# A decoder layer with 32 experts on one core: the first tile of each expert is made inside the attention

## The chip, the cores and the metric

The kernel runs on one core of a Trainium2 chip. The metric is the device time of one execution in microseconds (us); the median of several runs is given. Before the change it is 585.74 us (nine runs, 582.87 to 588.87).

## The reference, cut to what matters

The layer takes x of 16 sequences (blocks) of 128 tokens with 256 features, a context of the same shape and a mask, and does three things, each with a layer norm in front and a residual add behind:

```
x = x + latent_attention(layernorm(x))          # 32-wide compressed q, k, v with rotary tables
x = x + cross_attention(layernorm(x), ctx)      # 32 heads of 8, 8 key groups, causal, masked
x = x + experts(layernorm(x))

# experts, over all 2048 tokens
probs = softmax(h @ gate.T)                     # 32 experts
top_vals, top_idx = top_k(probs, 8)
# keep the largest until their renormalised sum reaches 0.8; shares rw sum to 1
for each expert e:                              # FF = 96
    g, u = split(h @ gate_up[e].T)
    out += (silu(g) * u) @ down[e].T * share[:, e]
```

A token keeps at most six experts with these inputs, so most token and expert pairs are zero. All arrays are float32.

## The kernel before

**Attention.** The kernel's first part is a loop over steps `t`, with an order of instructions written out by hand (`tc.manual_schedule`): each engine executes its instructions in the order in which the loop issues them. Four steps make one block of 128 tokens. In a step `step(t)` makes the score tiles (lines 561 to 587): those of the first pass go to `nmz`, the row maxima (DVE, line 581), those of the second pass, which run LAG = 5 steps later, through an exponential to `pt` (ACT, line 586). `maxima(b)` transposes the maxima of block b at t = 4b + 4 and adds them to the queries (`q8m`, DVE, line 536; once per block, so its starts tell the length of four steps). `weigh`, `divide` and `project` follow for the block's two halves (`o_ps` line 594, `ot_ps` line 612, `y_ps` line 634). `values` copies the block's values on POOL (`va`, line 526). Beside them generators are advanced piece by piece with `piece`: latent attention and queries of the next group of four blocks (`ahead`), keys (`side`), and `route` of the finished blocks (`routing`). The last step with scores is t = 66; with `last` = 65 the steps from 65 on are called the tail here. PSUM has three banks with tag `mm` for all small products, four with tag `s` for scores and one with tag `o`.

**Routing.** `route(b0, nb)` works on two blocks at a time, the last four blocks singly. It normalises the tokens (`rs_f`, a power on POOL, line 291; then DVE, PE `tp_f`), makes the logits, the kept experts (`kept`, DVE), and the rank of each token within its expert: a product of `kept` with a triangular matrix plus the running count `before` (`r_ps`, lines 711 to 720). From the rank it takes the row number `di` = expert x 2048 + rank. Then seven indirect DMAs for each block, called sends here (`send`, POOL, line 749), write the token's row of 292 numbers (256 features, token number, 32 shares) to that row of the DRAM buffer `xs`. The sends wait in the list `waiting` and are issued two in a step, three from step 65 on. S11.1 below means block 11, its send number 1.

**SP's queue.** SP issues, in order, loads and the list `bulk`, three in a step from t = 4: zeroing of the first 128 rows of each expert in `xs` (32 transfers of 146 KB), zeroing of the three accumulators `acc` (48), and the weights `wgu` (32). At t = 68 the attention's buffers are given back (`gctx.close`) and `load_down` loads the down weights `wdn` into them.

**Setup of the expert part.** From `before` a short chain (lines 928 to 999) computes how many rows each expert has, the list of tiles beyond the first of each expert (`lrow`, `lexp`), and masks `valid` of the rows in use.

**Expert loop.** The 32 first tiles (rows 0 to 127 of each expert) are written out; the further tiles follow in chunks of CHUNK = 8, nested in `tc.If(n_more > c * CHUNK)`. At each chunk the engines load the tiles' row and expert numbers into registers (line 1093). A tile is 128 rows: SP loads it (`xt`, six ahead), PE transposes it (`x_ps`, line 1031), ACT copies (`xT`), PE multiplies with gate and up weights (`g`, line 1040), ACT makes Silu (`sg`, line 1049), DVE multiplies (`h`, line 1051), PE transposes `h` (line 1058), DVE copies (`hT`, line 1060), PE multiplies with `wdn` (`y_ps`, line 1071), DVE scales with the share (`y`, line 1075), and POOL adds the rows to the accumulator by an indirect DMA, called an add here:

```
nc.gpsimd.indirect_dma_start(
    out=acc[i % NACC],
    out_offset=bass.IndirectOffsetOnAxis(ap=slot[:, i : i + 1], axis=0),
    in_=y, in_offset=None, bounds_check=B * P - 1, oob_is_err=False,
    compute_op=ALU.add,
)
```

`slot` holds the token numbers; for rows not in use it holds 2048, beyond the bound, and such rows are left out (`copy_predicated`, line 1062). Three accumulators take turns. In `step(i, ...)` PE's order is: half of the next tile's gate product, transpose of this `h`, transposes of the tile three ahead, the other half of the next gate product, this tile's `y_ps`.

**End.** The accumulators are read back, added to x and stored (lines 1137 to 1154).

Of the kernel before, what the change touches and what calls it, by code (L numbers as in the profile page):

```python
# [18 lines left out]
P = 128  # L19
B = 16  # L20
# [16 lines left out]
R_TOK, R_SHARE = D, D + 1  # L37
NX = B * P * TOPK // P
CHUNK = 8
AHEAD = 6  # L40
NACC = 3
# [5 lines left out]
C_TRI, C_ONE, C_SEL, C_IOTA, C_EB = 840, 968, 1096, 1608, 1736  # L47
C_TRI32, C_JROW, C_CAND, C_P, C_JX, C_J1, C_P1 = 1768, 1800, 1816, 1820, 1821, 1822, 1823
C_END = 1824
# [15 lines left out]
def decoder_layer(  # L65
# [47 lines left out]
    tab = const.tile([P, C_END], F32, tag="tab", name="tab")  # L113
# [22 lines left out]
    nc.vector.memset(zero, 0.0)  # L136

# [12 lines left out]


# [6 lines left out]
    with ExitStack() as actx:  # L158
# [3 lines left out]
        tbuf = ctx.enter_context(tc.tile_pool(name="tbuf", bufs=2))  # L162
        gctx = ExitStack()
# [39 lines left out]
        wf = apool.tile([P, GB, D], F32, tag="wf", name="wf")  # L203
# [3 lines left out]
        def fold():  # L207
# [38 lines left out]

            for j in range(GB):
                nc.scalar.activation(wf[:, j, :], wf_ps, AF.Copy, scale=bm4[:, j : j + 1])
# [80 lines left out]
        def latent_attention(g):  # L329
# [93 lines left out]
            for j in range(0, GB, 2):  # L423
                y_ps = mm([P, 2, D], f"ly_ps_{g}_{j}")
                for i in range(2):
                    nc.tensor.matmul(  # L426
                        y_ps[:, i, :], lhsT=on, rhs=wf[:, j + i, :], start=True, stop=True
                    )
                nc.vector.tensor_tensor(
                    xres[:, b0 + j : b0 + j + 2, :], y_ps, xres[:, b0 + j : b0 + j + 2, :], ALU.add  # L430
                )
            yield
# [206 lines left out]
        def route(b0, nb):  # L639
# [94 lines left out]
            for j in range(nb):  # L734
# [8 lines left out]
            nc.vector.tensor_tensor(  # L743
                row[:, :, R_SHARE : R_SHARE + NE], kept,
                sk.unsqueeze(2).to_broadcast([P, nb, NE]), ALU.mult,
            )

            def send(j, k):
                sent = nc.gpsimd.indirect_dma_start(  # L749
                    out=xs, out_offset=bass.IndirectOffsetOnAxis(ap=di[:, j, k : k + 1], axis=0),  # L750
                    in_=row[:, j, :], in_offset=None,
                    bounds_check=ROWS - 1, oob_is_err=False,
                )

                tc.declare_no_dep(sent.ins, group="sent", reason="rows are distinct")
                tc.add_to_no_dep_group("sent", sent.ins)


            for j in range(nb):
                for k in range(TOPK - 1):  # L760
                    waiting.append((pair, lambda j=j, k=k: send(j, k)))

        def load_down():
# [7 lines left out]
            return wdp, wdn  # L771
# [34 lines left out]
        nc.sync.dma_start(out=tab[:, C_FIRST:], in_=table[:, C_FIRST:])  # L806
# [18 lines left out]
        bulk = [(xs[e * CAP : e * CAP + P, :], zero) for e in range(NE)]  # L825
# [5 lines left out]
        waiting, rows, turn = [], {}, [0]  # L831

        routed = {b: (b - 1, 2) for b in range(1, B - 4, 2)}
        routed.update({b: (b, 1) for b in range(B - 4, B)})
# [9 lines left out]

        values(0)
        t = 0
        while t < 4 * B + LAG + 8 or behind or routing or fresh:
# [21 lines left out]
            if t == last + 3:  # L869

                gctx.close()
                wdp, wdn = load_down()
# [29 lines left out]
            if t % 4 == 1 and t // 4 + 1 < B:  # L902
                values(t // 4 + 1)
            piece(side)
# [3 lines left out]
            onward()  # L908
            for _ in range(3):
# [3 lines left out]
            for _ in range(2 if t < last else 3):  # L913
# [6 lines left out]
        while waiting:  # L920
            waiting.pop(0)[1]()

# [6 lines left out]
    pcol = tab[:, C_P : C_P + 1]  # L929
    valid = wdp.tile([P, NE + NX], I32, tag="valid", name="valid")  # L930
    n_ps = pp.tile([P, NE], F32, tag="x", name="n_ps")
    nc.tensor.matmul(n_ps, lhsT=ones, rhs=before, start=True, stop=True)
    nc.vector.tensor_scalar(valid[:, 0:NE], n_ps, pcol, None, ALU.is_gt)


# [6 lines left out]
        more[:, 1:16], tab[0:NE, C_JROW + 1 : C_JROW + 16], np2[:, 0:1], None, ALU.is_lt  # L942
    )
    xt = wdp.tile([NE, 1], F32, tag="xt", name="xt")
    nc.vector.tensor_reduce(xt, more[:, 1:16], AX.X, ALU.add)
    t_ps = pp.tile([NE, 2], F32, tag="h", name="t_ps")
    nc.tensor.matmul(
        t_ps[:, 0:1], lhsT=tab[0:NE, C_TRI32 : C_TRI32 + NE], rhs=xt, start=True, stop=True
# [6 lines left out]
    for q in range(4):  # L955
        nc.tensor.matmul(
            q_ps[:, q, :], lhsT=tab[0:NE, C_SEL + q * P : C_SEL + (q + 1) * P], rhs=np2,
# [7 lines left out]
        pos, nq[:, :, 0], tab[:, C_JX : C_JX + 1], 9999.0, ALU.is_le, ALU.mult  # L965
    )
    nc.vector.tensor_tensor(pos, pos, nq[:, :, 1], ALU.add)
    nc.vector.tensor_scalar(pos, pos, tab[:, C_J1 : C_J1 + 1], None, ALU.add)
# [3 lines left out]
    nc.vector.tensor_scalar(low, nq[:, :, 0], -1.0, tab[:, C_JX : C_JX + 1], ALU.mult, ALU.add)  # L972
    nc.vector.tensor_scalar(low, low, float(P), 0.0, ALU.add, ALU.max)
    row0 = wdp.tile([P, 4], F32, tag="row0", name="row0")
    nc.vector.tensor_tensor(row0, tab[:, C_CAND : C_CAND + 4], low, ALU.subtract)
    hot = wdp.tile([P, 4, NX], F32, tag="hot", name="hot")
    for q in range(4):
        nc.vector.tensor_scalar(
            hot[:, q, :], tab[:, C_IOTA : C_IOTA + NX], pos[:, q : q + 1], None, ALU.is_equal
# [8 lines left out]
    nc.vector.tensor_scalar(valid[:, NE:], v_ps, tab[:, C_P1 : C_P1 + 1], None, ALU.is_gt)  # L988
# [12 lines left out]
    slot = wdp.tile([P, NE + NX], I32, tag="slot", name="slot")  # L1001
# [44 lines left out]
    def gate_tile(i):  # L1046
        v = held[i]
        sg = hbuf.tile([P, FF], F32, tag="sg", name=f"sg_{i}")
        nc.scalar.activation(sg, v["g"][:, 0:FF], AF.Silu)  # L1049
        v["h"] = h_ring[i % len(h_ring)]  # L1050
        nc.vector.tensor_tensor(v["h"], v["g"][:, FF:], sg, ALU.mult)  # L1051

    def step(i, e_dve, e_next, row_ahead):
        v = held[i]
        if i + 1 < NT:
# [4 lines left out]
        nc.vector.tensor_copy(hT, h_ps)  # L1060

        nc.vector.copy_predicated(  # L1062
# [201 lines left out]
```

## Time and profile before

| what | value |
|---|---|
| median of nine runs | 585.74 us (582.87 to 588.87) |
| the profiled execution, its own time | 588.16 us |
| its span in the profile | 586.3 us, mean granted clock 0.874 |
| busy: PE, DVE, ACT, POOL | 456.4, 344.7, 175.8, 289.8 us |
| last score step ends, about | 348 us |
| last send starts | 390.8 us |
| adds of the expert loop, first and last start | 404.2 and 552.9 us |
| end of the span | 586.3 us |

The page of a profile describes one execution. Part 2 cuts the span into 40 slices of 14.66 us and gives the busy share of each engine in tenths. Part 5 lists groups of instructions: line, engine, operation, tile written and tiles read, count, then busy us and mean ns of one, then the engine's idle time in front of them and what ended it. A timeline lists instructions in order of time: start, duration in us, engine, line, operation. A window's line has its limits and length and the busy us of PE, weight loads (PEld), DVE, ACT and POOL with the counts, then the mean granted clock of PE, the share of the DMA engines in use, and GB/s.

### The profile page before, as it was taken

To read this page: it belongs to the slowest core of one execution; us is meant where nothing else is said; L and a number is where in the kernel's file an instruction comes from. 1 tells how busy PE (TensorE), PEld (TensorE's weight loads), DVE (VectorE), ACT (ScalarE), POOL (GpSimd) and SP (SyncE) were. 2 spreads that over 40 slices of the span, in tenths; PEclk is the share of its full clock that TensorE was granted. 3 is DMA by queue.
4 is the path that set the end of the run, shared out by engine and by line. 5 is a ranking of instruction groups with operands and counts; after the bars stand their busy time and mean duration, and the time that the engine had idled before them with its cause. 6 is when DMAs were issued, how large, how long until landed. Compare 5 with 4: busy or idle time off the path is not lost.

```text
span 586.3 us, 11946 instructions
## 1 busy us (share of the span) xinstructions
PE 456.4 (78%) x4168; PEld 328.5 (56%) x4168; DVE 344.7 (59%) x1168; ACT 175.8 (30%) x436; POOL 289.8 (49%) x295
## 2 busy tenths in 40 slices
PE   4979788998699888989989883349888888888500
PEld 3646475665466555666756533237666667776400
DVE  3464466576765776665757754624555545665456
ACT  2121033444225433443434341004233222332100
POOL 5711220011264272645446357753888887888700
PEclk9978679999799998996979797558999988998955
DMA  8200267423720718601111119223666577788388
GB/s 268 97 1 28 53 150 183 130 87 87 228 96 30 240 52 186 217 27 33 35 38 37 34 35 244 80 65 105 120 123 122 113 131 136 140 148 141 67 277 297
DMA packets 62743, 68.62 MB, mean 117 GB/s; under 512 B 12962, under 2 KB 57000, under 8 KB 62384
## 3 DMA queue, kind: packets, MB, share of 16 engines
q1 hardware_dynamic: 43232, 50.01, 30.3%
q0 software_dynamic: 16896, 14.98, 14.1%
q10 hardware_dynamic: 2544, 2.75, 1.4%
q8 instruction: 36, 0.59, 0.4%
q14 instruction: 35, 0.29, 0.2%
HBM read 37.48 MB, written 42.50 MB: 136 GB/s over the span
## 4 chain that ended last, share of the span: by engine, by line
PE 40%; DMA 17%; DVE 15%; issue 13%; POOL 11%; SPq 2%; ACT 1%; POOLq 0%; DVEq 0%
POOL xs L749 6%; PE g L1040 6%; DMA acc<-y,slot 6%; PE y_ps L1071 5%; PE s_ps L561 5%; DVE nmz L581 4%; DMA part<-acc 4%; PE o_ps L594 3%; PE s_ps L567 3%; PE q_ps L503 3%; DMA q<-qd 2%; PE x_ps L1031 2%; PE s_ps L574 2%; PE ly_ps L426 1%; DMA xs<-zero 1%
## 5 line engine op out<-in xcount | busy, mean ns | idle before, releaser
L1078 POOL DMA_INDIRECT acc<-y,slot x80 | 123.9, 1549 | 38.7 <-DVE slot L1062 15.4
L749 POOL DMA_INDIRECT xs<-row,di x112 | 110.4, 985 | 36.4 <-issue 29.9
L581 DVE TENSOR_REDUCE nmz<-s_ps 128x4 f32<-128x512 f32 x128 | 82.4, 686 | 66.2 <-PE s_ps L574 63.7
L586 ACT ACTIVATE pt<-s_ps 128x512 f32<-128x512 f32 x128 | 69.5, 595 | 107.3 <-PE s_ps L574 103.3
L1040 PE MATMUL g<-wgu,xT 128*128 (+1 forms) x324 | 83.4, 341 | 10.6 <-issue 10.6
L561 PE MATMUL s_ps<-k,q 32*128 32x128 f32 x1024 | 87.6, 305 | 0.0
L567 PE MATMUL s_ps<-q8m,k 32*128 32x512 f32 x256 | 79.9, 702 | 6.4 <-DVE q8m L536 3.3
L561 PEld LDWEIGHTS s_ps<-k,q 32*128 32x128 f32 x1024 | 74.6, 206 | 3.2 <-issue 1.1
L1033 ACT COPY xT<-x_ps 128x256 f32<-128x256 f32 x83 | 30.9, 372 | 124.0 <-PE x_ps L1031 103.2
L1040 PEld LDWEIGHTS g<-wgu,xT 128*128 128x128 f32 x324 | 58.0, 201 | 17.4 <-issue 13.0
L1071 PE MATMUL y_ps<-wdn,hT 96*128 (+1 forms) x160 | 57.0, 439 | 8.4 <-DVE hT L1060 8.1
L1075 DVE TENSOR_SCALAR y<-y_ps,xt 128x256 f32<-128x256 f32 x80 | 38.7, 484 | 23.1 <-DMA acc<-y,slot 8.4
L1051 DVE TENSOR_TENSOR h<-g,sg 128x96 f32<-128x96 f32 x81 | 20.7, 256 | 38.6 <-ACT sg L1049 28.9
L567 PEld LDWEIGHTS s_ps<-q8m,k 32*128 32x128 f32 x256 | 21.9, 198 | 36.3 <-issue 23.0
L594 PE MATMUL o_ps<-pt,va 128*32 128x512 f32 x256 | 39.0, 686 | 1.8 <-DVE xres L637 1.8
L1031 PE MATMUL x_ps<-tab,xt 128*128 128x128 f32 x166 | 33.8, 287 | 6.1 <-DMA xt<-xs 6.1
L1071 PEld LDWEIGHTS y_ps<-wdn,hT 96*128 96x128 f32 x160 | 25.2, 195 | 21.2 <-DVE hT L1060 14.1
L526 POOL COPY va<-v_sb 128x64 f32<-128x64 f32 x16 | 3.7, 233 | 65.4 <-PE o_ps L594 65.4
L600 ACT ACTIVATE ot<-o_ps,tab 128x512 f32<-128x512 f32 x32 | 22.1, 689 | 31.4 <-PE o_ps L594 31.3
L1060 DVE COPY hT<-h_ps 96x128 f32<-96x128 f32 x80 | 22.7, 284 | 12.4 <-PE h_ps L1058 12.2
L1031 PEld LDWEIGHTS x_ps<-tab,xt 128*128 128x128 f32 x166 | 21.4, 147 | 8.5 <-DMA xt<-xs 6.3
L1058 PE MATMUL h_ps<-tab,h 128*96 128x128 f32 x80 | 22.8, 285 | 0.4 <-DVE h L1051 0.4
(216 smaller groups left out, 696.6 us busy)
## 6 DMA issues: line engine op xcount, KB each, us to landing
xt<-xs SPq DMA_DIRECT2D x86, 146.0 KB
acc<-zero SPq DMA_DIRECT2D x48, 128.0 KB
wgu<-in_w_gu_t SPq DMA_DIRECT2D x32, 192.0 KB
part<-acc SPq DMA_DIRECT2D x24, 256.0 KB
xs<-zero SPq DMA_DIRECT2D x32, 146.0 KB
ct<-in_ctx_t SPq DMA_DIRECT2D x4, 512.0 KB
qd<-qt SPq DMA_DIRECT2D x8, 256.0 KB
out<-xres ACTq DMA_DIRECT2D x8, 256.0 KB
```

The costliest lines, as they stand in the source:

```text
L561: nc.tensor.matmul(s_ps[:, i, :], lhsT=q8[g % 2][rows, i, tok], rhs=k8[g % 2][h][rows, tok], start=(i == 0), stop=True, skip_group_check=True,
L567: nc.tensor.matmul(s_ps, lhsT=k8[g % 2][h][rows, tok], rhs=q8ms[b][rows, :, :], start=True, stop=True, skip_group_check=True,)
L581: nc.vector.tensor_reduce(nmz[b % 2][:, :, 32 * r + h], s_ps, AX.X, ALU.max, negate=True)
L586: nc.scalar.activation(pt, s_ps, AF.Exp)
L594: nc.tensor.matmul(o_ps[32 * r : 32 * r + 32, :, :], lhsT=vaug[b % NVA][:, 4 * h + r, :], rhs=pts.pop((b, h, r)), start=True, stop=True,)
L749: sent = nc.gpsimd.indirect_dma_start(out=xs, out_offset=bass.IndirectOffsetOnAxis(ap=di[:, j, k : k + 1], axis=0), in_=row[:, j, :], in_o ...
L1031: nc.tensor.transpose(x_ps[:, c, :], v["xt"][:, c * P : (c + 1) * P], ident)
L1033: nc.scalar.copy(v["xT"], x_ps)
L1040: nc.tensor.matmul(v["g"], lhsT=v["xT"][:, c, :], rhs=wgu_flat[:, bass.ds(v["e"] * W2 + c * NE * W2, W2)], start=(c == 0), stop=(c == KC - 1),
L1071: nc.tensor.matmul(y_ps, lhsT=hT, rhs=wdn[:, bass.ds(v["e"] * D, D)], start=True, stop=True)
L1075: nc.vector.tensor_scalar(y, y_ps, v["xt"][:, bass.ds(e_dve + R_SHARE, 1)], None, ALU.mult)
L1078: nc.gpsimd.indirect_dma_start(out=acc[i % NACC], out_offset=bass.IndirectOffsetOnAxis(ap=slot[:, i : i + 1], axis=0), in_=y, in_offset=No ...
```

## The change

The first tile of each expert is now made of the tokens of the first eight blocks alone (NEARLY = 8), while the attention still runs.

- When the sends of blocks 0 to 7 are all issued (56 of them), the generator `early()` is advanced once per step, and twice from step 65 on. One advance is a slot (`first_slot`): it loads a tile two slots ahead (`load_first`, with that expert's down weights), and does a part of three tiles: y product and add for tile i - 2, gate products and gating for tile i - 1, transposes for tile i. There are 34 slots for 32 tiles. Here the gate products give `h` already transposed, so that no transpose of `h` is needed. Adds A0 to A31 go to POOL among the sends: A0 in step 51, A13 in step 64, A14 and A15 in step 65, A30 and A31 in step 73.
- After block 7 is routed, the running count is raised to at least 128 for each expert, so that rows of later tokens begin behind the first tile. Blocks 6 and 7 are routed singly for this. The first 256 rows of each expert are zeroed, and the token number in a zeroed row is 2048.
- The expert loop then handles the second tile of each expert (32, written out) and the list of third and later ones, in chunks of CHUNK = 4. `copy_predicated` remains for the listed tiles.
- `gated` takes the place of Silu and one multiply: silu(g) u = 0.5 (tanh(g / 2) + 1) g u, with tanh on ACT and two DVE operations; the factor 0.5 is put into the shares.
- Sends of blocks 0 to 7 go out four in a step after step 32, and all sends four in a step from step 65 on.
- A part of the table is loaded later, with the down weights (`tab2`), and `wf` is a quarter as large: in the latent attention the four `ly_ps` products use 32 rows each in place of 128 rows with zeros.

```diff
+    def add_rows(i, y, tokens):
+        nc.gpsimd.indirect_dma_start(
+            out=acc[i % NACC],
+            out_offset=bass.IndirectOffsetOnAxis(ap=tokens, axis=0),
+            in_=y, in_offset=None, bounds_check=B * P - 1, oob_is_err=False,
+            compute_op=ALU.add,
+        )
+    def gated(pool, g, u, name, h):
+        th = pool.tile(g.shape, F32, tag="th", bufs=2, name=f"th_{name}")
+        nc.scalar.activation(th, g, AF.Tanh, scale=0.5)
+        a = pool.tile(g.shape, F32, tag="ga", bufs=2, name=f"ga_{name}")
+        nc.vector.scalar_tensor_tensor(a, th, 1.0, g, ALU.add, ALU.mult)
+        nc.vector.tensor_tensor(h, a, u, ALU.mult)
...
+            if b0 + nb == NEARLY:
+                yield
+                n_ps = mm([P, NE], "n_ps_first")
+                nc.tensor.matmul(n_ps, lhsT=ones, rhs=before, start=True, stop=True)
+                nc.vector.tensor_scalar(before, n_ps, float(P), 1.0 / P, ALU.max, ALU.mult)
...
-        bulk = [(xs[e * CAP : e * CAP + P, :], zero) for e in range(NE)]
+        bulk = [(xs[e * CAP : e * CAP + 2 * P, :].rearrange("(k p) r -> p k r", p=P),
+                 zero.unsqueeze(1).to_broadcast([P, 2, RW])) for e in range(NE)]
...
+        def load_first(e):
+            v["xt"] = ebuf.tile([P, RW], F32, tag="ext", bufs=SOON + 4, name=f"ext_{e}")
+            load = nc.sync.dma_start(out=v["xt"], in_=xs[e * CAP : e * CAP + P, :])
+            v["wd"] = ebuf.tile([FF, D], F32, tag="ewd", bufs=SOON + 3, name=f"ewd_{e}")
+            nc.sync.dma_start(out=v["wd"], in_=w_dn_t[:, e, :])
...
+        def first_slot(i):
+            if i + SOON < NE:
+                load_first(i + SOON)
+            if i >= 2:
+                v = first_tiles[i - 2]
+                y_ps = mm([P, D], f"ey_ps_{i - 2}")
+                nc.tensor.matmul(y_ps, lhsT=v["h"], rhs=v["wd"], start=True, stop=True)
+                y = ebuf.tile([P, D], F32, tag="ey", bufs=3, name=f"ey_{i - 2}")
+                nc.scalar.mul(y, y_ps, v["xt"][:, R_SHARE + v["e"] : R_SHARE + v["e"] + 1])
+                add_rows(i - 2, y, v["xt"][:, R_TOK : R_TOK + 1].bitcast(I32))
+            both_ps = mm([P, 2, KC, P], f"eg_ps_{i}")
+            if 1 <= i <= NE:
+                v = first_tiles[i - 1]
+                g_ps = both_ps[0:FF, 1, :, :]
+                for f in range(2):
+                    for c in range(KC):
+                        nc.tensor.matmul(
+                            g_ps[:, f, :], lhsT=wgu[:, c, v["e"], f * FF : (f + 1) * FF],
+                            rhs=v["xT"][:, c, :], start=(c == 0), stop=(c == KC - 1))
+                v["h"] = ebuf.tile([FF, P], F32, tag="eh", name=f"eh_{i - 1}")
+                gated(ebuf, g_ps[:, 0, :], g_ps[:, 1, :], f"e{i - 1}", v["h"])
+            if i < NE:
+                v = first_tiles[i]
+                for c in range(KC):
+                    nc.tensor.transpose(both_ps[:, 0, c, :], v["xt"][:, c * P : (c + 1) * P], ident)
+                v["xT"] = ebuf.tile([P, KC, P], F32, tag="exT", name=f"exT_{i}")
+                nc.scalar.copy(v["xT"], both_ps[:, 0, :, :])
...
+            if count[0] == NEARLY * (TOPK - 1):
+                piece(soon, "mm" if t < last + 2 else "s")
...
             onward()
+            if t >= last:
+                piece(soon, "mm" if t < last + 2 else "s")
...
-            for _ in range(2 if t < last else 3):
+            n = 2
+            if t >= last or waiting and 4 * NEARLY < t and waiting[0][0] < NEARLY // 2:
+                n = 4
+            for _ in range(n):
                 if waiting:
                     waiting.pop(0)[1]()
...
-        nc.scalar.activation(sg, v["g"][:, 0:FF], AF.Silu)
-        nc.vector.tensor_tensor(v["h"], v["g"][:, FF:], sg, ALU.mult)
+        gated(hbuf, v["g"][:, 0:FF], v["g"][:, FF:], f"{i}", v["h"])
...
-        nc.vector.copy_predicated(
-            slot[:, i : i + 1], valid[:, i : i + 1], v["xt"][:, R_TOK : R_TOK + 1].bitcast(I32)
-        )
+        if i >= NE:
+            j = i - NE
+            nc.vector.copy_predicated(slot[:, j : j + 1], valid[:, j : j + 1], tokens)
+            tokens = slot[:, j : j + 1]
...
-        row_of = lambda i: i * CAP if i < NE else first_rows[i - NE]
+        row_of = lambda i: i * CAP + P if i < NE else first_rows[i - NE]
```

## The prediction

> **What bounds the kernel now.** I read the page's slices first (part 2), then its costliest groups (part 5), POOL's timeline from 150 us to the end, DVE's timeline and the window sums for the attention, the timeline of all engines in the expert loop, and the waits last. In the slices, 14.66 us each:
>
> ```profile
> PE   4979788998699888989989883349888888888500
> POOL 5711220011264272645446357753888887888700
> PEclk9978679999799998996979797558999988998955
> ```
>
> PE is full until slice 23 (350 us) and POOL is half idle; then PE drops to 3 and its clock to 0.5 while POOL stays at 7; from slice 27 both are at 8. The groups:
>
> ```profile
> L1078 POOL DMA_INDIRECT acc<-y,slot x80 | 123.9, 1549 | 38.7 <-DVE slot L1062 15.4
> L749 POOL DMA_INDIRECT xs<-row,di x112 | 110.4, 985 | 36.4 <-issue 29.9
> ```
>
> In POOL's timeline (start, us, line, operation, idle time before it) these two run without a hole from the attention's last steps on:
>
> ```profile
> 346.44 1.17 POOL L749 DMA_INDIRECT xs<-row,di  x1 [0.20 <-issue]
> ...
> 390.82 0.97 POOL L749 DMA_INDIRECT xs<-row,di  x1 [0.30 <-issue]
> 404.17 1.60 POOL L1078 DMA_INDIRECT acc<-y,slot  x1 [12.38 <-DVE slot L1062]
> ...
> 502.39 1.55 POOL L1078 DMA_INDIRECT acc<-y,slot  x1 [0.30 <-DVE h L1051]
> 504.25 1.55 POOL L1078 DMA_INDIRECT acc<-y,slot  x1 [0.30 <-issue]
> ...
> 552.89 1.55 POOL L1078 DMA_INDIRECT acc<-y,slot  x1 [0.30 <-issue]
> ```
>
> A send holds POOL 0.97 + 0.30 = 1.277 us, an add 1.55 + 0.30 = 1.855 us, whatever the rows hold: L1078's shortest is 1.539, its longest 1.601, and experts with one token are among the 80. The 34 sends from 346.4 to 391.8 are those of steps 65 and later (S11.1 to S15.6). So after step 65 POOL sets the end twice: in the tail (45.4 us) and in the expert loop (404.17 to 552.89 for 79 adds, 1.883 us each).
>
> **Tiles.** The reference's router on its own inputs gives 72 non-empty tiles, 42 beyond an expert's first; in eights that is 48, and 32 + 48 = 80 is the x80 above. After, an expert holds max(rows of the first 1024 tokens, 128) plus the rest: 31 third or later tiles, 32 in fours. So 32 early tiles, 32 second, 32 later: 96 adds, of which 64 in the loop.
>
> **1. The expert loop.** 16 adds fewer at 1.883 are -30.1 us if POOL stays the bound. PE's own loop, from the timeline of all engines:
>
> ```profile
> 497.52 0.26 DVE L1051 TENSOR_TENSOR h<-g,sg 128x96 f32<-128x96 f32 x1 [0.42 <-ACT sg L1049]
> 497.90 0.27 PE L1058 MATMUL h_ps<-tab,h 128*96 128x128 f32 x1
> 498.23 0.49 PE L1040 MATMUL g<-wgu,xT 128*128 x2
> 498.75 0.25 ACT L1049 ACTIVATE sg<-g 128x96 f32<-128x96 f32 x1
> 499.04 0.26 DVE L1051 TENSOR_TENSOR h<-g,sg 128x96 f32<-128x96 f32 x1 [0.42 <-ACT sg L1049]
> ```
>
> h, its transpose, the next gate matmul, the activation, the next h: 1.52 us round, a chain of latencies. `gated` puts a second DVE step into it; by h's row 0.26 + 0.04 (bounds: 0.20, the one-column copy, and 0.48, a scalar_tensor_tensor of 256 columns). 1.82 is still under 1.855, so the 32 second tiles stay POOL's. The loop in chunks waits at each boundary (waits: total us, times, longest):
>
> ```profile
> PEld g L1040 <- issue: 13.0, 6, 2.4
> ```
>
> There PE loads its expert numbers (L1093: 0.32 us for one value, 2.13 for eight: 0.26 a value, so 1.09 for four). A chunk of four: 4 x 1.82 + 1.09 = 8.37 against POOL's 7.42; over 8 chunks 7.6, less the 2.3 us by which the last y leads the last add (550.6 to 552.89): +5.3. Bounds: 0, and +15.7 if a load of four costs as much as one of eight. Taken -30.1 + 5.3 = **-25** (-30 to -14). The 202 ns of `copy_predicated` that 32 tiles lose hide behind POOL: 0.
>
> **2. The start.** Between last send and first add lie 12.4 us; an ACT_TABLE_LOAD of 1.28 us (397.87) for Silu is in it, and DVE's second step costs 0.3. Taken **-1** (-1.3 to +0.3, where tanh needs a load too). The Trainium skill (ScalarE: Activation LUTs, What ACT_TABLE_LOAD costs) gives 1283 ns plus about 1380 of drain for a switch; the copy before this load ends at 397.85, 0.02 us ahead, so the row shows no drain; by the page the term would be -2.4.
>
> **3. The tail.** In the changed program's POOL order the adds A14 to A31 stand among the same 34 sends, two per step from step 65. POOL needs 34 x 1.277 + 18 x 1.855 + 2 for the small ones = 78.8 against 45.4: **+33.4** with nothing waiting, and this is a floor, as before had no hole to fill. On top: (a) SP. Tile 22's load waits for the buffer that A16 holds (6 buffers), about 16 us in; `load_down` stands behind it (3.4 MB with tab2, at the 241 GB/s of 360 to 370 us 14 us), and tile 24's load behind that: about 34 us in, while its add is due at 44 and the next one's matmuls sit behind its transposes on PE. (b) The route chains of blocks 14 and 15: rs_f(14) to rs_f(15) took 8.8 us, from there to di(15) 8.9; with 4 and 6 slots of about 2 us in between 17 and 21, against POOL's 13 and 20 meanwhile: up to 5. Behind a waiting add on POOL stand sends and rs_f, and PE waits for the latter. Taken **+37** (+33 to +46).
>
> **4. The attention's steps.** By step 65 PE has 16 slots more. A slot is 2 transposes and 8 passes of 128 columns (107 ns each: the 16 passes of c_ps take 1.71) and 2 passes of 256 (213: y_ps L634, four in 0.85): 1.50 us at full clock, 1.67 at the 0.9 of this stretch. What a step has free is read from DVE's timeline, one q8m for each block of four steps:
>
> ```profile
> 277.83 0.68 DVE L536 SCALAR_TENSOR_TENSOR q8m<-mt_ps,q 128x512 f32<-128x512 f32 x1
> 291.39 0.68 DVE L536 SCALAR_TENSOR_TENSOR q8m<-mt_ps,q 128x512 f32<-128x512 f32 x1
> 308.41 0.68 DVE L536 SCALAR_TENSOR_TENSOR q8m<-mt_ps,q 128x512 f32<-128x512 f32 x1
> ```
>
> and in the sums of the window 250 to 300 us (length; busy us of PE, weight loads, DVE, ACT and POOL; clock; DMA):
>
> ```profile
> 250.00:300.00 50.00, 45.12 (x563) 31.65 (x563) 32.32 (x113) 19.44 (x38) 20.68 (x27) 0.85 0.09 28
> ```
>
> A block takes 13.6 or 17.0 us; the long ones hold a 2 us wait of r_ps for DVE and a half-clock stretch after it. PE is busy 45.1 of 50, so 0.38 us of a step is idle. All slots on top: +27. With that idle time used, 1.3 us each: +21. The 8 slots of long blocks free as well (they fit the waits), the others 1.1: +9. I take **+15**, between the last two, as every second block has such a wait. DVE (32 of 50, +0.56 a slot), ACT (19, +1.1) and POOL (21, +1.855 for A0 to A13) hide their parts; if POOL's cover goes, va copies and rs_f queue behind an add, 1.9 us per step. The rest: blocks 6 and 7 routed singly (one more chain on DVE, about 3 us), zeroing doubled (4.7 MB more at the 200 GB/s of 80 to 100 us, 23 us of transfers behind which SP's next load, at 109, is wanted only some steps later: 0, else 8), ly_ps with 32 rows instead of 128 (0 to -5), early sends four a step (POOL idle: 0). Together +2 (-4 to +9). Taken **+17** (+5 to +32).
>
> Sum: -25 - 1 + 37 + 17 = +28. The profiled execution took 588.2 (span 586.3), so 616; the median of nine is 2.4 lower, so **614**.
>
> **Rivals.** (B) *Slots stall PE.* PE runs in order and a slot takes two of three `mm` banks, so a bank that ACT or DVE frees late stops the scores too: 2.5 us per slot instead of 1, +24 more: 638. For it: the chains cross four engines per slot; against: DVE and ACT are 40 to 60% idle. (C) *Slots hide wholly*, and the loop keeps POOL's pace: +33.4 - 30.1 - 1 + 2 = +4: 590. For it: the idle 10% and the waits; against: 13.6 us blocks have no 6 us to give. (D) *Faster: step 65 comes earlier.* PE stands at half clock for some 24 us between 274 and 343, each stretch behind a wait. If slots fill those waits, the clock holds, 12 us of the stretches come back, and ly_ps gives 3 to 5; with all slots hidden the sum is +4 - 16 = -12: 574. It decides once q8m's spacing falls below 3.6 us a step (now 60.7 / 16 = 3.79), since the tail and loop cost at least +2.3 by POOL alone. The Trainium skill (TensorE: Matmul & The Clock Gate, The HAM clock gate) says an idle window of about 3.4 us halves the clock, and the half-clock stretches here are 3.4 to 10 us long; by that rule fillers help, but the waits seen are 2 us.
>
> **How the numbers follow.** Forecast 0.62 (own range 602 to 628), B 0.17, C 0.11, D 0.10. Range 590 to 640: it leaves out D and the ends of B and C. What this kernel's measurement can tell from no change is about 0.3%, 1.8 us. Faster 0.11 (D and a rest of C), same 0.03, slower 0.86.
>
> **Right or wrong.** Right: x96 for the adds at 1.55 us; last send to the first add of the loop about 11.5; the loop about 125 us; POOL without holes for some 80 us before it; q8m's spacing 4.7 to 5 us in its last four blocks; no second table load. Wrong: adds of empty tiles shorter than 1.5 us, holes on POOL in the tail, a first add of the loop before 440 us (I expect 457), or a spacing under 4 us.

## The result, and the profile after

The changed kernel takes 640.84 us (median of 20 runs, 632.77 to 651.27) against 585.88 us of the kernel before beside it. Some of its executions are in a slower state; the fast ones have a median of 637.95 us, and the ratios here are of fast ones: 1.0888, 95% interval 1.0862 to 1.0915. It is slower, as forecast, but by 52 us instead of 28, near the upper end of the range (590 to 640). The profiled execution has a span of 638.3 us (clock 0.894), 52.0 more than before. The stages, read from POOL's timelines of both profiles:

| stage | before | after | difference | forecast |
|---|---|---|---|---|
| attention, to the first send or add of step 65 | 346.4 | 385.2 | +38.8 | +17 |
| tail, to the end of the last send | 45.4 | 86.4 | +41.1 | +37 |
| last send's end to the loop's first add | 12.4 | 9.9 | -2.5 | -1 |
| loop, first to last add | 148.7 | 123.8 | -25.0 | -25 |
| end | 33.4 | 32.9 | -0.5 | 0 |

The slices of the page after are now 15.96 us each:

```profile
PE   4877899986998888897877886656629988888700
POOL 5611120021743727532565356767746878777700
PEclk9959779997999979879999689969759999999955
```

From slice 18 (290 us), where the slots begin, PE falls to 7 and 8, although work was added to it; then to 6 and 5 in the tail. The groups of the page after, POOL's sends and adds (early, second tiles, listed tiles):

```profile
L157 POOL DMA_INDIRECT acc<-ey,ext x32 | 50.8, 1588 | 42.1 <-ACT ey L907 33.1
L769 POOL DMA_INDIRECT xs<-row,di x112 | 111.3, 994 | 36.1 <-issue 30.6
L157 POOL DMA_INDIRECT acc<-y,xt x32 | 49.5, 1546 | 21.4 <-DVE y L1173 11.6
L157 POOL DMA_INDIRECT acc<-y,slot x32 | 49.4, 1543 | 14.9 <-DVE hT L1157 12.3
```

The counts (96 adds, 64 of them in the loop) and prices are those of the forecast. POOL's timeline after:

```profile
385.24 1.64 POOL L157 DMA_INDIRECT acc<-ey,ext  x1 [0.36 <-ACT th_e L167]
...
419.23 1.54 POOL L157 DMA_INDIRECT acc<-ey,ext  x1 [3.59 <-ACT th_e L167]
...
470.68 0.98 POOL L769 DMA_INDIRECT xs<-row,di  x1 [0.30 <-issue]
481.59 1.56 POOL L157 DMA_INDIRECT acc<-y,xt  x1 [9.93 <-DVE y L1173]
...
605.35 1.54 POOL L157 DMA_INDIRECT acc<-y,slot  x1 [0.30 <-DVE y L1173]
```

In the tail POOL now has holes (3.59 us and smaller ones). The largest miss is ahead of it: DVE's timeline, `q8m` of the blocks 11, 12, 13 and 15, shows blocks of 18.4 to 29.7 us where they took 13.4 to 17.0:

```profile
280.10 0.68 DVE L554 SCALAR_TENSOR_TENSOR q8m<-mt_ps,q 128x512 f32<-128x512 f32 x1
298.45 0.68 DVE L554 SCALAR_TENSOR_TENSOR q8m<-mt_ps,q 128x512 f32<-128x512 f32 x1
321.89 0.68 DVE L554 SCALAR_TENSOR_TENSOR q8m<-mt_ps,q 128x512 f32<-128x512 f32 x1
...
374.87 0.69 DVE L554 SCALAR_TENSOR_TENSOR q8m<-mt_ps,q 128x512 f32<-128x512 f32 x1 [1.62 <-PE mt_ps L551]
```

Block 11 starts 2.3 us later than before (277.83). That agrees with the "rest" of +2 but does not show it: in five kernels with the same attention as before it starts anywhere from 272.1 to 277.8. The stretch from block 11 to block 15 is firmer, 58.3 to 61.9 us in those five. Here it takes 94.8 us instead of 60.7: 16 slots cost 34 us, 2.1 each, where 0.94 was forecast. PE is not full in that stretch, as the window sums of after show (busy us of PE, weight loads, DVE, ACT, POOL; clock; DMA):

```profile
300.00:350.00 50.00, 37.90 (x479) 28.19 (x477) 28.05 (x99) 20.94 (x49) 29.99 (x30) 1.00 0.33 76
```

37.9 of 50 us, at full clock. What it waits for stands in the waits of after (us in all, times, longest), and one slot of the timeline shows it in place:

```profile
PE eg_ps L924 <- DVE eh L170: 42.0, 31, 6.7
```

```profile
322.70 1.04 PE L915 MATMUL eg_ps<-exT,wgu 128*96 128x128 f32 x8
323.84 0.27 ACT L167 ACTIVATE th_e<-eg_ps 96x128 f32<-96x128 f32 x1 [0.47 <-ACT ey L907]
324.14 0.28 DVE L169 SCALAR_TENSOR_TENSOR ga_e<-th_e,eg_ps 96x128 f32<-96x128 f32 x1 [0.75 <-ACT th_e L167]
324.46 0.28 DVE L170 TENSOR_TENSOR eh<-ga_e,eg_ps 96x128 f32<-96x128 f32 x1
324.80 0.44 PE L924 MATMUL eg_ps<-tab,ext 128*128 128x128 f32 x2 [1.06 <-DVE eh L170]
325.16 0.70 PE L585 MATMUL s_ps<-q8m,k 32*128 32x512 f32 x2
```

The gate products end at 323.74. Tanh and the two DVE steps read them until 324.74. Only then do the transposes of the next tile (L924) start, 1.06 us after PE had become free, and the scores (L585) stand behind them. The transposes do not need `eh`: they read another tile. But they write `both_ps[:, 0]`, the other half of the tile `both_ps` whose half 1 the gating is still reading, and the program makes PE wait for those readers. Theory W, then: the slot costs this wait, not its matmuls. (Of the 42.0 us, 19.0 lie ahead of the tail, in 15 waits, and 23.0 in it. The longest, 6.7, is a special case: in it ScalarE itself waited for an add.) The rivals: (M) the slot's matmuls fill PE; (P) the adds on POOL hold back what the attention needs from POOL.

### The profile page after: what moved, and what is told of

Same layout as the page of the kernel before. It is cut to its first block, busy times and chain, and to the rows that moved or that the text cites. A ratio compares the mean times of both kernels' runs of the same rounds, so it can differ in the third digit from the quotient of the medians.

```text
span 638.3 us, 12696 instructions
## 1 busy us (share of the span) xinstructions
PE 486.8 (76%) x4410; PEld 341.8 (54%) x4410; DVE 360.2 (56%) x1233; ACT 201.0 (31%) x498; POOL 316.8 (50%) x312
## 3 DMA queue, kind: packets, MB, share of 16 engines
q0 software_dynamic: 19200, 15.00, 13.6%
## 4 chain that ended last, share of the span: by engine, by line
PE 42%; DVE 20%; DMA 13%; issue 8%; POOL 7%; ACT 7%; SPq 1%; POOLq 0%; DVEq 0%; ACTq 0%
PE s_ps L579 6%; DVE nmz L599 4%; PE s_ps L585 4%; PE o_ps L612 4%; POOL xs L769 3%; DMA acc<-ey,ext 3%; DMA part<-acc 3%; ACT xT L1131 3%; PE h_ps L1155 3%; PE x_ps L1129 3%; PE q_ps L521 2%; PE s_ps L592 2%; DVE ga L169 2%; ACT th L167 2%; DVE h L170 2%
## 5 line engine op out<-in xcount | busy, mean ns | idle before, releaser
L585 PE MATMUL s_ps<-q8m,k 32*128 32x512 f32 x256 | 79.3, 708 | 5.1 <-DVE q8m L554 2.7
L157 POOL DMA_INDIRECT acc<-ey,ext x32 | 50.8, 1588 | 42.1 <-ACT ey L907 33.1
L1138 PE MATMUL g<-wgu,xT 128*128 128x192 f32 (+1 forms) x260 | 65.2, 334 | 6.2 <-issue 5.3
L157 POOL DMA_INDIRECT acc<-y,xt x32 | 49.5, 1546 | 21.4 <-DVE y L1173 11.6
L157 POOL DMA_INDIRECT acc<-y,slot x32 | 49.4, 1543 | 14.9 <-DVE hT L1157 12.3
L1138 PEld LDWEIGHTS g<-wgu,xT 128*128 128x128 f32 x260 | 44.5, 194 | 12.2 <-ACT th L167 5.6
L924 PE MATMUL eg_ps<-tab,ext 128*128 128x128 f32 x64 | 14.9, 316 | 42.0 <-DVE eh L170 42.0
L169 DVE SCALAR_TENSOR_TENSOR ga<-th,g 128x96 f32<-128x96 f32 x65 | 16.5, 254 | 51.6 <-ACT th L167 51.6
L1169 PE MATMUL y_ps<-wdn,hT 96*128 96x256 f32 (+1 forms) x128 | 44.2, 427 | 0.1
L1129 PE MATMUL x_ps<-tab,xt 128*128 128x128 f32 x134 | 26.5, 281 | 14.4 <-DMA xt<-xs 14.3
L915 PE MATMUL eg_ps<-exT,wgu 128*96 128x128 f32 x256 | 36.5, 289 | 0.8 <-ACT xnt_f L343 0.4
L915 PEld LDWEIGHTS eg_ps<-exT,wgu 128*96 128x96 f32 x256 | 33.0, 174 | 6.6 <-ACT exT L928 3.2
L585 PEld LDWEIGHTS s_ps<-q8m,k 32*128 32x128 f32 x256 | 21.6, 201 | 26.4 <-issue 18.2
L924 PEld LDWEIGHTS eg_ps<-tab,ext 128*128 128x128 f32 x64 | 6.7, 146 | 49.9 <-DVE eh L170 49.1
```

The lines of the kernel that those rows point to most:

```text
L157: nc.gpsimd.indirect_dma_start(out=acc[i % NACC], out_offset=bass.IndirectOffsetOnAxis(ap=tokens, axis=0), in_=y, in_offset=None, bounds_c ...
L585: nc.tensor.matmul(s_ps, lhsT=k8[g % 2][h][rows, tok], rhs=q8ms[b][rows, :, :], start=True, stop=True, skip_group_check=True,)
L915: nc.tensor.matmul(g_ps[:, f, :], lhsT=wgu[:, c, v["e"], f * FF : (f + 1) * FF], rhs=v["xT"][:, c, :], start=(c == 0), stop=(c == KC - 1),)
L1129: nc.tensor.transpose(x_ps[:, c, :], v["xt"][:, c * P : (c + 1) * P], ident)
L1138: nc.tensor.matmul(v["g"], lhsT=v["xT"][:, c, :], rhs=wgu_flat[:, bass.ds(v["e"] * W2 + c * NE * W2, W2)], start=(c == 0), stop=(c == KC - 1),
L1169: nc.tensor.matmul(y_ps, lhsT=hT, rhs=wdn[:, bass.ds(v["e"] * D, D)], start=True, stop=True)
```

## The experiments

**Transposes first.** All PE writes of the shared tile come ahead of all reads; nothing is added or removed.

```diff
             both_ps = mm([P, 2, KC, P], f"eg_ps_{i}")
+            if i < NE:
+                for c in range(KC):
+                    nc.tensor.transpose(
+                        both_ps[:, 0, c, :], first_tiles[i]["xt"][:, c * P : (c + 1) * P], ident
+                    )
             if 1 <= i <= NE:
...
             if i < NE:
                 v = first_tiles[i]
-                for c in range(KC):
-                    nc.tensor.transpose(
-                        both_ps[:, 0, c, :], v["xt"][:, c * P : (c + 1) * P], ident
-                    )
                 v["xT"] = ebuf.tile([P, KC, P], F32, tag="exT", name=f"exT_{i}")
```

> The changed kernel with one edit in the slot: PE transposes tile i into its half of the PSUM tile before it makes the gate products of tile i-1 in the other half, so that every PE write of that tile is ahead of every read; no instruction is added or left out. Theory W (in the changed kernel the transposes wait until the gating chain has read the other half, about 1.36 us for each of 31 slots, and the scores queue behind them): the 16 slots ahead of the tail lose about 1.3 us each, so the tail begins near 364 us instead of 385, the tail is 80 to 86 us instead of 86.7, and the time is 614 to 621. Rival M (the slot's own matmuls fill PE): no change, 638 to 643, tail from 383 to 387. Rival P (the adds on POOL hold back the sends and the other POOL work that the attention waits for): no change here either.

Measured: 615.43 us, ratio to before 1.0479 (1.0398 to 1.0559). The tail begins at 360.5 us, 24.8 earlier, and lasts 83.9, 2.5 less. No wait of the transposes for `eh` is left among the waits, and in its window sums PE is nearly full:

```profile
300.00:350.00 50.00, 48.65 (x600) 37.80 (x601) 31.37 (x104) 26.71 (x64) 35.97 (x37) 0.94 0.38 90
```

Block 11 to block 15 now takes 74.6 us, +13.9 over before: 0.87 us per slot. W holds; M falls, since the matmuls are the same. Two things belong beside that number. The mean granted clock from block 11 to 15 is 0.89 before, 0.92 after and 0.95 here, so the better clock is in it: the kernel before would have taken 56.9 us at 0.95, if all of the stretch followed the clock, an estimate by which the slots alone cost up to 1.1 each. And the false wait is not gone altogether: ScalarE's copy of the transposed half now waits for DVE's read of the other half, though both only read; no PE instruction stands right behind that copy:

```profile
ACT exT L929 <- DVE eh L170: 21.5, 25, 1.6
```

**No early adds.** The 32 adds of the first tiles are left out, everything else of a slot stays.

```diff
-                add_rows(i - 2, y, v["xt"][:, R_TOK : R_TOK + 1].bitcast(I32))
```

> The changed kernel without the 32 adds of the first tiles on POOL; all the rest of a slot stays, and the first tiles' results are left out of the output. Theory W: the attention does not wait for these adds, so the tail begins at 383 to 387 us as before the edit; the tail loses POOL's 33.4 us only as far as PE and the routes allow, 50 to 62 us instead of 86.7; time 604 to 617. Rival M: the same start of the tail. Rival P: the tail begins 15 to 30 us earlier (355 to 370) and lasts about 46; time 570 to 590.

Measured: 629.45 us, 1.0741 (1.0680 to 1.0802). The tail begins at 384.9 us, as with the adds, so P falls: POOL did hide A0 to A13. But the tail still takes 76.2 us (384.85 to 461.03) with POOL idle for 31 us of it. Taking away 33 us of work on the engine that I had called the tail's bound gave back 10. W was right on the attention and wrong on the tail (50 to 62 expected).

**Both.** Was that remainder the false wait? The two edits above together.

> The changed kernel with both edits, transposes first and no adds of the first tiles on POOL (their results are left out), to see what the tail costs PE without the false wait and without POOL's adds. If the 76 us of the tail without adds were the waits of PE for the gating chain, 18 slots of 1.36 us go: tail 46 to 60 us, start of the tail 357 to 362, time 578 to 594. Rival (the routes of the last blocks and the tile loads behind the down weights keep PE, whatever the slots wait for): tail 68 to 78 us, time 598 to 608.

Measured: 604.98 us, 1.0268 (1.0195 to 1.0341). The tail takes 73.4 us (359.93 to 433.32); the rival holds. In POOL's timeline of this kernel the route of the last block comes 20 us after the send before it:

```profile
389.67 0.97 POOL L769 DMA_INDIRECT xs<-row,di  x1 [0.30 <-issue]
409.85 0.57 POOL L311 TENSOR_TENSOR rs_f<-ve_f,mhalf 128x1 f32<-128x1 f32 x1 [19.21 <-DVE ve_f L309]
```

Within these 20 us PE also waits once for the load of a first tile:

```profile
PE eg_ps L911 <- DMA ext<-xs: 7.6, 2, 7.4
```

SP asked for that tile at 375.96, right behind the down weights (373.60), and PE waited for it until 392.28; from 390 to 400 us the granted clock is 0.50. So the tail has two limits close together: POOL's 78.8 us of work, and about 73 us for the last blocks' routes behind two slots per step, this wait beside the weights included. How much of the 73 belongs to each is not shown.

**Tanh alone.** The kernel before, with `gated` in its loop and the shares halved.

```diff
-        sg = hbuf.tile([P, FF], F32, tag="sg", name=f"sg_{i}")
-        nc.scalar.activation(sg, v["g"][:, 0:FF], AF.Silu)
         v["h"] = h_ring[i % len(h_ring)]
-        nc.vector.tensor_tensor(v["h"], v["g"][:, FF:], sg, ALU.mult)
+        gated(hbuf, v["g"][:, 0:FF], v["g"][:, FF:], f"{i}", v["h"])
```

> The kernel before with the tanh form of silu alone (shares halved, one more DVE step in the gating). Theory: the loop stays bound by POOL (PE's round 1.52 + 0.30 = 1.82 us against an add's 1.855), so first to last add stays at 148 to 150 us, and the start loses 1 us (by the load's row alone) to 2.7 us (what the changed kernel showed): 583 to 585. Rival: the longer chain makes PE the bound, at about 1.95 us a tile: loop 154 us or more, 588 to 592. By the Trainium skill's page ScalarE: Activation LUTs the start would lose 2.4 us.

Measured: 595.41 us, 1.0166 (1.0123 to 1.0210): a miss. First to last add takes 157.1 us instead of 148.7. The round itself is the predicted one, as the transposes of `h` in this kernel's timeline of all engines show:

```profile
421.43 0.31 PE L1064 MATMUL h_ps<-tab,h 128*96 128x128 f32 x1
423.25 0.31 PE L1064 MATMUL h_ps<-tab,h 128*96 128x128 f32 x1
```

1.82 us. What I had left out of this expectation is the boundary term of my own prediction: 8 x 1.82 + 2.13 = 16.7 us for a chunk of eight against POOL's 14.8, over six boundaries 11, less the 2.3 us of lead: +8.8; measured +8.4. A round just under POOL's pace has nothing left with which to make up a boundary. Before, eight rounds of 1.52 us and the load were 14.3, just under POOL's 14.8.

**Silu in the loop again.** On top of the transposes first; the early slots keep tanh.

```diff
-        gated(hbuf, v["g"][:, 0:FF], v["g"][:, FF:], f"{i}", v["h"])
+        sg = hbuf.tile([P, FF], F32, tag="sg", name=f"sg_{i}")
+        nc.scalar.activation(sg, v["g"][:, 0:FF], AF.Silu)
+        nc.vector.tensor_tensor(v["h"], v["g"][:, FF:], sg, ALU.mult)
...
-            y, y_ps, v["xt"][:, bass.ds(e_dve + R_SHARE, 1)], None, ALU.mult
+            y, y_ps, v["xt"][:, bass.ds(e_dve + R_SHARE, 1)], 2.0, ALU.mult, ALU.mult
```

> The changed kernel with transposes first, and in the loop alone the old Silu (the factor of two rides in the last scaling); the early slots keep tanh. Boundary term: PE's four rounds and the load fall from 4 x 1.82 + 1.09 = 8.37 to 4 x 1.52 + 1.09 = 7.17, under POOL's 7.42, so first to last add goes from 124.2 to 118 to 120 us; the start gains back a table load (0.3 to 2.7 us longer): 609 to 613 against 615.4. Rival: the holes at the boundaries are not PE's rounds (POOL's or DVE's own register loads): loop 123 to 125 us, time 615 to 618.

Measured: 610.06 us, 1.0397 (1.0338 to 1.0457). The whole time is not told apart from the 1.0479 (1.0398 to 1.0559) of the kernel it was made from; the stage shows it. First to last add takes 118.5 us instead of 124.2, so the boundaries cost 5.7 us (forecast 5.3), and POOL alone takes 30.2 us off the loop (forecast 30.1). The start does not change, 10.6 us in both, though a table load of 1.28 us is back.

**Smaller chunks in the kernel before.** CHUNK = 4, and CHUNK = 2.

```diff
-CHUNK = 8
+CHUNK = 4    # and 2
```

> The kernel before with the tiles beyond an expert's first in fours instead of eights: 76 tiles instead of 80. If POOL stays the bound over the boundaries (four rounds of 1.52 us and a load of 1.09 are 7.17, against POOL's 7.42): 4 x 1.855 = 7.4 us less, loop 141 us, time 577 to 580. Rival (each boundary leaves POOL a hole of about 0.8 to 1.1 us, as in the changed kernel): 11 holes give 9 to 12 us back, 586 to 591.

> The kernel before with the tiles beyond an expert's first in twos: 74 tiles instead of 80. If POOL stays the bound (two rounds of 1.52 us and a load of two values, about 0.58, are 3.62 against POOL's 3.71): 6 x 1.855 = 11.1 us less than before, 3.7 less than with chunks of four: 571 to 576. Rival: 21 boundaries take more than PE's lead can give (each 0.5 us of POOL idle): the gain over fours is eaten, 577 to 588.

Measured: fours 576.78 us, 0.9862 (0.9816 to 0.9908); twos 574.28 us, 0.9774 (0.9731 to 0.9817). 76 and 74 adds, first to last in 142.5 and 136.5 us. The waits of the kernel with twos show that PE meets 20 boundaries and that none is longer than 0.6 us (before: six of up to 2.4):

```profile
PE g L1040 <- issue: 7.2, 20, 0.6
```

This is a version that beats both kernels: it removes six adds of empty tiles and moves nothing else.

**An add ahead of the loop.** In the kernel before with fours, one accumulating DMA whose rows are all skipped, in step 52.

```diff
+            if t == 52:
+                nc.vector.memset(none, B * P)
+                nc.gpsimd.indirect_dma_start(
+                    out=acc[0], out_offset=bass.IndirectOffsetOnAxis(ap=none, axis=0),
+                    in_=zero[:, 0:D], in_offset=None, bounds_check=B * P - 1, oob_is_err=False,
+                    compute_op=ALU.add,
+                )
```

> The kernel before in chunks of four, with one more accumulating indirect DMA from POOL in the attention's step 52, all of whose rows are skipped. Reading to be tried: in kernels with no add ahead of the loop the first add starts 2.05 to 2.15 us after the end of its y, in those with early adds 0.27, so a program's first add costs some 1.9 us before it starts. If so, the first add starts 0.3 us after y, the stretch from the last send to the first add falls from 12.0 to 10.1 us and the time by 1.9, to 573 to 576. Rival (the 2.1 us belong to the wait for the tile of row numbers): the stretch stays at 12 us and the time at 576 to 578.

Measured: 578.85 us, 0.9856 (0.9807 to 0.9906), the same as without it. The first add still starts 2.14 us after its `y` (398.84 to 400.98). My reading falls. What shortens this step to 0.27 us in the kernels with early adds is not found.

**Earlier slots.** The kernel with transposes first and Silu in the loop, first tiles from six blocks (`NEARLY = 6`), so that 24 slots instead of 16 lie ahead of the tail.

```diff
-NEARLY = 8
+NEARLY = 6
```

> The changed kernel with transposes first and the old Silu in the loop (610.06 us so far), and the first tiles are those of the first six blocks instead of eight (again 32 tiles in the list), so that eight more slots lie ahead of the tail. If a slot in the attention costs about 0.75 us and an add or a slot in the tail 1.6 to 1.9: attention +6 to +8, tail 84 to 66-72 us, time 600 to 606. Rival (slots cost as much ahead of the tail as in it, or the tail is held by the last blocks' routes alone): 608 to 613.

Measured: 610.42 us, 1.0394 (1.0321 to 1.0467), no change. The tail falls from 83 to 71 us, but the attention grows by 10 (1.2 us a slot, 9.6 for eight) and the loop by 3.5, for a reason not looked into. Moving slots ahead trades one place for the other.

**The hole in the tail.** After transposes first, POOL's largest hole is 5.15 us. Around it the core's engines stand still for six microseconds but for the end of one add, as the windows show (same columns):

```profile
382.00:388.00 6.00, 1.49 (x13) 1.23 (x11) 0.00 (x0) 0.00 (x0) 4.48 (x6) 1.00 1.05 267
388.00:394.00 6.00, 0.00 (x0) 0.00 (x0) 0.00 (x0) 0.50 (x2) 1.10 (x1) 0.53 0.87 222
```

ScalarE's waits in this kernel name what it waits for, and the view of the adds' line tells how long an add takes to land:

```profile
ACT ey L907 <- DMA acc<-ey,ext: 13.8, 2, 11.6
```

```profile
DMA to landing us min/median/max: 2.8/3.8/13.6
```

First I tried the queue: the weights asked for three steps later.

```diff
                 gctx.close()
+            if t == last + 6:
                 wdp, wdn, tab2 = load_down()
```

> The changed kernel with transposes first (615.43 us so far), and the 3.4 MB of down weights are asked for three steps later, so that the early tiles' loads are not queued behind them on SP. If POOL's hole of 5.15 us in the tail is those loads: the hole falls under 1 us, the tail from 83.9 to 79 to 80 us, time 609 to 612. Rival (the hole is PE's turn of the last blocks' routes): the tail stays at 82 to 85, time 614 to 617; were the weights then late for the loop, its first add would come later by up to 6 us.

Measured: 623.82 us, 1.0630 (1.0559 to 1.0702), 8 us slower; a miss. Not all of it is the weights: the tail is 6.4 us longer, but it also begins 5.2 later, 3.7 of them already there at the first block's `q8m`, and the loop is 1.9 shorter. The hole is not gone, it is 8.77 us and moved with the weights. In this kernel ScalarE's longest wait for an add is 10.4 us, and it ends at 425.38, 16.9 us after SP asked for the weights (408.44); in the kernel before this edit 17.4 us after (376.14 to 393.50), in the changed kernel 15.4 (403.09 to 418.48). The buffers `ey` are three, so `ey` of one tile waits for the landing of the add three earlier, and that landing is the long one: from the add's start to the end of the wait it is 14.9 us with transposes first (378.61 to 393.50), 13.3 in the changed kernel (405.15 to 418.48) and 14.0 with the later weights (411.40 to 425.38), while 3.1 MB of weights are moving; the view, which has the landing of only some of the adds, has 3.8 as the median. Then all edits so far together: transposes first, Silu in the loop, six blocks, weights three steps later.

> The changed kernel with all four edits: transposes first, old Silu in the loop, first tiles of six blocks, down weights three steps later. If the terms add up (-5 for the loop, -4 to -10 for the six blocks, -4 to -5 for the weights): 596 to 602, still above the 586 of the kernel before, since the early adds cost POOL and PE in the tail more than the loop gives back. Rival (the terms are one and the same wait in the tail): 602 to 608.

Measured: 608.82 us, 1.0374 (1.0306 to 1.0442). The terms did not add up; with fewer slots in the tail SP asked for the weights only 1.9 us later, and the hole (4.62 us) stayed.

**Weights in pieces.** Transposes first, and eight pieces of 0.39 MB, one per step from t = 68.

```diff
-                wdp, wdn, tab2 = load_down()
+            if last + 3 <= t < last + 11:
+                load_down(t - last - 3)          # experts 4 k to 4 k + 3
```

> The changed kernel with transposes first (615.43 us so far), and the 3.1 MB of down weights asked for in eight pieces of 0.39 MB, one per step of the tail, instead of all at once. Reading to be tried: in the tail ScalarE's ey waits 11.6 us for the landing of an earlier add, which comes only when the weights are in, all engines stop with it, and asking for the weights later only moves that wait. If so, each piece holds an add back by some 2 us, which the ring of three ey covers: POOL's hole of 5.15 us falls under 2, the tail from 83.9 to 79 to 81, time 609 to 613. Rival (an add needs 10 us to land whenever weights are moving): the wait comes in several shorter pieces of the same sum, tail 83 to 86, time 614 to 619.

Measured: ratio 1.0383 (1.0311 to 1.0455); in this run the kernel before took 652.66 us beside it, so absolute times do not compare. By the ratio alone it is not told apart from the 1.0479 (1.0398 to 1.0559) without pieces. The trace is: ScalarE's one wait for an add is 2.3 us, POOL's longest hole in the tail 1.95, and the tail is 81.7 us. The pieces did not all leave one per step: the last four were issued together (477.72 to 479.17), and the wait of 2.3 us that is left is for the add started beside them (477.87).

```profile
ACT ey L911 <- DMA acc<-ey,ext: 2.3, 1, 2.3
```

## Why the prediction was half right, step by step

**Loop, -25: right in both parts.** POOL's 16 adds gave -30.2 and PE's boundaries took 5.7 back. POOL's pace (1.855), PE's round (1.82) and the load of the expert numbers (median 1.07 us for four, 1.09 priced) were each measured as priced. One bound of the range was mis-sized: a load of four that cost as much as one of eight would make +13.6 by the same rows, not +15.7.

**Start, -1: the sum was near, the reason wrong.** -2.5 was measured. The tanh kernel, which removes the same table load alone, has a start 0.6 us longer, which is within the scatter of the kernels with the start of before (12.0 to 12.95), and putting Silu back costs 0.0. The Trainium skill (ScalarE: Activation LUTs, What ACT_TABLE_LOAD costs) with its drain would have given -2.4; that it lies near the -2.5 is chance, as these two runs show no gain from the switch at all. Most of the difference, 1.87 of the 2.5, is in the distance from the first `y` to the first add, 2.14 us before and 0.27 after, whose cause stays open.

**Tail, +37: near in size, half of the cause.** Measured +41.1. POOL's floor of 78.8 us held. Step (a) had the wrong wait: tile 24's load does start 33.2 us into the tail (forecast about 34), but by luck. SP had issued the weights by 405.5, so the load did not stand behind them in its queue. It waited for its buffer, which an add started at 405.15 was still reading:

```profile
SPq L891 <- DMA acc<-ey,ext: 97.5, 26, 12.9
```

The add landed at 418.48, beside the weights. Tile 24's load started at 418.46, and ScalarE's `ey`, which waited for the same landing, at 418.48; the add of that `ey` ends POOL's hole of 3.59 us (415.64 to 419.23). The weights thus held an add back, not a load; asking for them later did not help and asking in pieces took most of the wait away. I called POOL the bound with nothing beside it; the runs without adds show that PE and the routes need 73 to 76 us without it, the wait for a tile's load beside the weights included. A cheaper add alone would have given little. With the false wait removed the tail is +38.6; that it agrees so well with +37 is partly luck, since one wait was put in the wrong place and the second limit left out.

**Attention, +17: this is the step that failed.** "A slot is ... 1.50 us at full clock", of which 0.94 would not fit into idle time: that priced the slot's matmuls, and with transposes first, when one slot takes 1.62 to 1.72 us on PE, they cost 0.87 per slot, the better clock included; the whole stage is then +14.0. (The 107 ns per pass of 128 columns in that working was read from `c_ps`, whose passes move 32 columns; the sum held all the same.) What I left out is a wait inside the slot. PE's order (gate products, then transposes into the same tile) stood in the diff and in the order of the changed program, and I wrote that DVE and ACT "hide their parts"; in fact their 1 us and more stood between two PE instructions, 31 times, 42 us in all. Taking the wait away starts the tail 24.8 us earlier and gives some 24 of the 52 us back (ratio 1.0479 instead of 1.0888): the kernel then takes 615.43 us, and the forecast was 614.

**Rivals.** B's price (2.5 us per slot, 638) was near to what happened, 2.1 per slot, but by another mechanism: not a bank of the `mm` ring freed late, but the other half of a tile that PE itself still fills. C and D fell: no slot was free, and the spacing of `q8m` rose to 5.9 us a step (3.79 before). Of D only the clock is seen, 0.89 before and 0.95 with transposes first from block 11 to 15. Of the signs by which the prediction was to be known as wrong, one showed: holes on POOL in the tail. The spacing, too, missed the 4.7 to 5 us that were to show it right.

The Trainium skill (PSUM — Partial Sum Buffer, PSUM bank collisions raise a hardware error) states the rule that the 42.0 us agree with: the compiler's back end puts a dependency between instructions of different engines that touch the same bank and the same 32 partitions, reads and writes alike, whatever bytes they touch. The copy that waits for DVE's read in the kernel with transposes first (21.5 us) agrees with it too. Whether the back end put these waits in or the program's own bookkeeping of tiles did, no run here shows. The rule names the wait that the prediction left out; its price is the 42.0 us of the trace.

## What to carry to other kernels

When two products share one PSUM tile, issue all the writes to it ahead of its first reader (tiles of their own, which no run here tried, may do as well); otherwise an in-order PE waits for a chain on two other engines that it does not need. Price moved work by what stands between its instructions as well as by their sum, and name the second limit behind the bound: here POOL (79 us) hid a chain of 73 (a wait of 7.4 for a tile's load in it). A pipeline stage that is made only slightly slower than the bound's pace can lose more than its own increase, because the reserve that made up interruptions is gone.

## What the runs showed of the hardware that was not expected

An add's rows, a transfer of 128 KB, landed in 3.8 us in the median, and in 13.3 to 14.9 us in three kernels while 3.1 MB of weights asked for by another engine were in flight; a tile's load took some 16 us to land beside them in a fourth. A ring of three buffers did not cover that. Eight pieces of 0.39 MB brought the wait down from 11.6 to 2.3 us, in a run that was slower altogether and with the last four pieces issued together. The first add behind the sends starts 2.04 to 2.15 us after its `y` in all kernels looked at without early adds or with a single one, and 0.27 us after it where 32 adds had gone before; why, no run tells.
